# Wo's weight sums of two sets moved to other slots and all onto VectorE, one of them in a buffer of its own; low rank copies put in front of statistics at the end

## The chip, the cores and the metric

The kernel runs on one core of a Trainium2 chip. The metric is the device time of one execution in microseconds (us). An engine is called by its name in the profile: PE is TensorE, PEld its weight loads, DVE is VectorE, ACT is ScalarE, POOL is GpSimd, and SP is the engine that issues most DMAs.

## What is computed

One transformer layer with the norm after each part, in float32, on x of shape (2, 512, 512): grouped attention with 32 heads of 128 in 8 groups, then a linear layer with low rank experts.

```python
q = rope(x @ Wq + bq); k = rope(x @ Wk + bk); v = x @ Wv + bv
scores = where(causal, q @ k.T / sqrt(128), min)        # 4 heads share one k and v
x = layernorm(x + softmax(scores) @ v @ Wo + bo)
y = x @ W_base.T + b_base
z = einsum('bth,erh->bter', x, lora_A[active])          # 4 experts, rank 8
alpha = softmax(log(prior) + x @ router_W.T + router_b)[active]
x = layernorm(x + y + sum over experts of (z @ lora_B.T * 2) * alpha)
```

## The kernel before

**Units, parts and slots.** The attention is cut into 16 units, a unit being one group of four heads in one batch. A unit has four parts of 128 query rows. A part is worked in four steps of 32 rows by four heads, so one step is one score matmul of 128 rows against 32 to 512 keys. These 256 steps are the slots 0 to 255, and the width grows by 32 from slot to slot through the 16 slots of a unit (the last unit has its parts in another order). The order of every engine's instructions is written out by hand: `slot(T)` (from L960) issues what belongs to slot T, and at its end whatever `put(T, f)` (L868) has stored for that slot. Nothing reorders it later. Each engine runs its own queue in order, and waits at an instruction until what it needs is there.

In slot T, PE does a product of the projections of a later unit, a product of Wo for an earlier one, the score of step T (L552), and the weighing by v of a part some 12 slots back (L608). DVE does the masked maximum of step T-1 (L560), adds the Wo product that PE has just left in PSUM to x (L666, "x_sb<-wx" and "x_sb<-wy"), adds the q product (L480), and then the reciprocal, the 32x32 transposes (L583, L585) and a piece of the rotary embedding (L374, L377, L381). ACT does the exponential (L567) and the scaling (L575), and copies from PSUM. POOL does the last addition of the rotary embedding (L382) and sums of four matrix blocks (L427 to L430).

**Wo and its sums.** Products with Wo are done with seven block products in place of eight, the Strassen way. Besides the weights they need three sums of weight blocks and one block changed in place: `wo_sums(n, step)`, steps 0 to 3 (L627 to L634), each one instruction over 128x512 elements. Wo comes in sets of four heads, `load_wo(n)`, 1 MB, two buffers. There are ten sets. Sets 0 to 5 serve two units each; the sets 6 to 9 serve one unit each, and only 6 and 7 are multiplied this way (8 and 9 use plain matmuls, L680). The sums live in one buffer with the tag "wt". With `wo_from(u)` = 16u + 21, the first slot of unit u's Wo products, the four steps are put at offsets 0, 1, 1, 3 from there for the sets 0 to 5, all on DVE. For the sets 6 and 7 they are at offsets -1, 0, 0, 0, that is in slots 212 and 213, and 228 and 229, with steps 0 and 1 on DVE and steps 2 and 3 on POOL. The load of set 7 is issued at slot 214.

The two PSUM banks of the Wo products are "wx" and "wy". Each has one buffer, so PE can start the next product in a bank only after DVE has added the former one to x.

**The end.** From slot 237 the slots also hold the first half of the linear layer, for the token tiles of batch 0 (`f0[0]` to `f0[3]`). W_base is transposed on PE in four pieces through the one buffer of `ps_k`, each copied out by ACT (`transposed_base`, put at 241, 242, 245 and 246). After that come, for each tile: `base` (PE, L774), `logits` and `alphas` (a small softmax on DVE and ACT), `low_rank` (PE transposes 32 columns into the `ps_k` buffer, L810, and DVE copies them to zT, L811), `finish` (PE multiplies zT by the low rank factors, L815), `add` (DVE adds x, L821, and takes the statistics, L699 and L700), the square root on ACT (L707), the reciprocal on DVE (L710), and `store` (POOL applies the norm, L729, and SP issues the DMA). The tiles of batch 1 follow in straight code behind the slots: `fa` (two tiles), `fb` and `fc`. `fc` is worked in two halves of columns (`half`, L829), with statistics of each half (L839).

Of the kernel before, what the change touches and what calls it, by code (L numbers as in the profile page):

```python
# [9 lines left out]
F32 = mybir.dt.float32  # L10
# [5 lines left out]
P = 128  # L16
# [13 lines left out]
def postln_layer_kernel(  # L30
# [33 lines left out]
    nc = tc.nc  # L64
# [8 lines left out]
    EAR = EA * RK  # L73
# [14 lines left out]
    NSETS = len(sets)  # L88

    def unit(u):  # L90
        return units[u]

    def set_of(u):
        return u // B if u < MIXED else MIXED // B + u - MIXED

    def set_units(n):
        return [u for u in range(NU) if set_of(u) == n]
# [5 lines left out]
    wow = ctx.enter_context(tc.tile_pool(name="wow", bufs=2))  # L103
# [3 lines left out]
    ps_k = ctx.enter_context(tc.tile_pool(name="ps_k", bufs=1, space=bass.MemoryType.PSUM))  # L107
# [52 lines left out]
    def load_wo(n):  # L160
        wo_g = wow.tile([P, R, HID], F32, tag="wo_g", name=f"wo_{n}")
        nc.sync.dma_start(out=wo_g, in_=Wo[ts(sets[n], R * D), :].rearrange("(r p) n -> p r n", p=P))
        wos[n] = wo_g
# [113 lines left out]
    def transpose_token_tile(dst, src, pool, tag, copy):  # L277

        tp = pool.tile([P, KC, P], F32, tag=tag, name="tp")
        for c in range(KC):  # L280
            nc.tensor.transpose(tp[:, c, :], src[:, ts(c, P)], ident)  # L281
        copy(dst, tp)
# [127 lines left out]
    CH = KC // 2  # L410
# [192 lines left out]
    def weigh(p, j):  # L603
        u, i = parts[p]
        g, b = unit(u)
        if j == 0:
            psc[p] = ps_ctx.tile([P, R, P], F32, tag="ctx", name="pc")
        nc.tensor.matmul(  # L608
            psc[p], lhsT=v_sb[g // VG, b][:, j, ts(g % VG, D)], rhs=pT[p][:, :, ts(j, P)],
            start=(j == 0), stop=(j == i))  # L610
# [8 lines left out]
    NHALF = HID // 2  # L619
    wt = {}  # L620
# [3 lines left out]
    def wo_block(n, c_half, n_half):  # L624
        return wos[n][:, CH * c_half : CH * (c_half + 1), ts(n_half, NHALF)]

    def wo_sums(n, step, engine=nc.vector):  # L627

        if step == 0:
            wt[n] = wow.tile([P, 3, CH, NHALF], F32, tag="wt", name=f"wt_{n}", bufs=1)  # L630
        t1, t2, t4 = (wt[n][:, m] for m in range(3))
        b11, b12, b21, b22 = (wo_block(n, c_half, n_half) for c_half in range(2) for n_half in range(2))
        engine.tensor_tensor(
            *((t1, b12, b11), (t2, b22, t1), (b12, b22, b12), (t4, b21, t2))[step], ALU.subtract)  # L634

    def ctx_block(k, head, c_half):
# [38 lines left out]
    def wo_mm(p, r):  # L675

        u, i = parts[p]
        if r == 0:
            pwo[p] = ps_wo.tile([P, HID], F32, tag=("wx", "wy")[p % 2], name="po")
        nc.tensor.matmul(  # L680
            pwo[p], lhsT=ctxT[p][:, r, :], rhs=wos[set_of(u)][:, r, :], start=(r == 0), stop=(r == R - 1))

    def wo_out(p):
        u, i = parts[p]
        t = unit(u)[1] * TPB + i
        nc.vector.tensor_tensor(x_sb[:, t, :], pwo[p], x_sb[:, t, :], ALU.add)
# [52 lines left out]
    class Ffn:  # L739
# [29 lines left out]
        def base(self, c):  # L769
            if c == 0:  # L770
                self.new_banks()
            for n in range(2):
                w = OH + (ARH, WX_COLS - OH)[n]
                nc.tensor.matmul(  # L774
                    self.py[n][:, :w], lhsT=self.xT[:, c, :], rhs=wbT[:, c, n, :w], start=(c == 0), stop=(c == KC - 1),
                    skip_group_check=True)
# [28 lines left out]
                    ALU.mult,  # L805
                )

        def low_rank(self):
            tz = ps_k.tile([EAR, P], F32, tag="k", name="tz")
            nc.tensor.transpose(tz, self.zs.rearrange("p a r -> p (a r)"), ident)  # L810
            nc.vector.tensor_copy(self.zT[:EAR], tz)  # L811

# [4 lines left out]
                    skip_group_check=True)  # L817

        def add(self):
            for n in range(2):  # L820
                nc.vector.tensor_tensor(self.y[:, ts(n, OH)], self.py[n][:, :OH], self.x[:, ts(n, OH)], ALU.add)  # L821
            self.norm2.stats(self.i, self.y)

        def half(self, n, c):

# [42 lines left out]
    def put(slot, f):  # L868
        extra.setdefault(slot, []).append(f)
# [39 lines left out]
    late = {}  # L909
    PERIOD = VG * B * UNIT  # L910
    for p in range(1, G // VG):
        at = PERIOD * p
# [16 lines left out]
    def wo_from(u):  # L929
        return UNIT * u + LAG_WO  # L930

    for n in range(2, NSETS):
        put(wo_from(set_units(n - 2)[-1] + 1) + 1, lambda n=n: load_wo(n))
    for n in range(NSETS - 2):
        single = len(set_units(n)) == 1
        for k in range(4):
            put(wo_from(set_units(n)[0]) + ((-1, 0, 0, 0) if single else (0, 1, 1, 3))[k],
                lambda n=n, k=k, engine=nc.gpsimd if single and k > 1 else nc.vector: wo_sums(n, k, engine))


    weigh_at = {}
# [133 lines left out]
    T_PROJ = T_END - 19  # L1075
# [13 lines left out]
    QX, QY, SC, CTX = (ps_q, "qx"), (ps_q, "qy"), (ps_sc, "sc"), (ps_ctx, "ctx")  # L1089

    def tiles(ts_, banks, name):
        n = len(ts_)
        norms = Norm(ffn_pool, n, f"a{name}"), Norm(ffn_pool, n, f"f{name}")
        return [Ffn(t, bank, *norms, i) for i, (t, bank) in enumerate(zip(ts_, banks))]

    f0 = tiles(range(TPB), ((QX, QY), (QX, QY), (SC, SC), (QX, QY)), "0")
    fa = tiles([TPB + i for i in order[:2]], ((SC, SC), (WX, WY)), "1a")
# [5 lines left out]
    def transposed_base(c):  # L1103
        transpose_token_tile(wbT[:, :, c // 2, ts(c % 2, P)], wb_sb[:, c, :], ps_k, "k", nc.scalar.copy)

    for c in range(OC):
        put(T_PROJ + (0, 1, 4, 5)[c], lambda c=c: nc.sync.dma_start(out=wb_sb[:, c, :], in_=W_base[ts(c, P), :]))
        put(T_PROJ + (4, 5, 8, 9)[c], lambda c=c: transposed_base(c))
    put(A - 5, lambda: f0[0].norm1.newton(0, 2))
    for k, f in enumerate(f0):  # L1110
        put(A + (-7, -6, 0, 0)[k], f.stats)
# [2 lines left out]
        put(A + 1 + k // 2, f.centre)  # L1114
        put(A + 3 + k // 2, lambda f=f, k=k: f.transpose(*(QX, QY)[k % 2]))
    for f, at in zip(f0, (A + 5, A + 11, A + 13)):
        for c in range(KC):
            put(at + c // 2, lambda f=f, c=c: f.base(c))
        put(at + 2, lambda f=f: (f.logits(), f.alphas()))
        put(at + 3, f.low_rank)  # L1120
        put(at + 4, lambda f=f: (f.finish(), f.add()))
    put(E + 2, fa[0].stats)
    for T in range(T_PROJ, E + 7):
        slot(T)
# [10 lines left out]
    fa[0].norm1.root(0, 2)  # L1135
    for f in fa:
        f.centre()
    f0[0].norm2.root(0, 3)
    for f in f0[:3]:
        f.store()  # L1140
    for r in range(R):
        wo_mm(NP - 2, r)
    wo_out(NP - 2)
    base(fz)
    fb.stats()
    fb.norm1.root(0, 1)
    fb.centre()
    for j in range(2):
        weigh(NP - 1, j)
    context_out(NP - 1)  # L1150
# [25 lines left out]
    fa[1].logits()  # L1176
    fa[1].alphas()
    fa[0].finish()
    fa[0].add()
    fa[0].norm2.sqrt(0, 1)  # L1180
    for c in range(KC):
        fb.base(c)
        if c == 2:
            fa[1].low_rank()
    fc.low_rank()
    fa[0].norm2.invert(0, 1)
    fa[0].store()
    fb.logits()
# [4 lines left out]
    for c in range(KC):  # L1193
        fc.half(0, c)
    fc.half_end(0)
    fc.half_stats(0)
    fa[1].norm2.invert(1, 2)
    fa[1].store()
    fb.low_rank()
    for c in range(KC):  # L1200
        fc.half(1, c)
        if c == 1:
# [58 lines left out]
```

## Time and profile before

| | |
|---|---|
| median of three runs | 827.23 us (824.42, 827.23, 827.54) |
| profiled execution, its own time | 824.35 us |
| its span, first to last instruction | 822.4 us |
| busy: PE, PEld, DVE, ACT, POOL | 812.3, 598.2, 600.6, 379.3, 326.7 us |
| mean granted TensorE clock | 0.999 |
| DMA queue of SP | 114.98 MB, 48.5% of 16 engines' span |

A timeline row has the start, the duration (both in us), the engine, the line, the operation, the tile written and the tiles read, the shape, and how many instructions were merged. In brackets stands the idle time before it, if there was any, and what ended it. Ends of matmuls are modelled and overlap the start of the next one, so time that PE loses is best read from start to start: four matmuls over 256 columns take 0.86 us from their start to the start of the next group when nothing is waited for (the program issues two, the profile records four).

### The profile page before, as it was taken

The page shows a single profiled execution, that of the slowest core. Times are in us where ns is not written, and L with a number is a line of the kernel's source. Part 1 is how long each engine was busy: PE and PEld are TensorE (multiplying, and loading weights), DVE is VectorE, ACT ScalarE, POOL GpSimd, SP SyncE. Part 2 cuts the span into 40 slices and gives each one's busy share as a digit, 9 for nine tenths or more (in the row PEclk, how much of TensorE's full clock was granted, in tenths as well). Part 3 has the DMA queues.
Part 4 walks back from the last instruction along what each step waited for, and adds up shares of the span by engine and source line. Part 5 has one row for each costly group of instructions (what it writes and reads, how often), then busy time and mean ns, then how long its engine had stood idle before and what let it go on. Part 6 is the DMA issues. An engine that isn't in the chain of part 4 may idle for free.

```text
span 822.4 us, 11201 instructions
## 1 busy us (share of the span) xinstructions
PE 812.3 (99%) x3385; PEld 598.2 (73%) x3385; DVE 600.6 (73%) x1968; ACT 379.3 (46%) x1058; POOL 326.7 (40%) x381
## 2 busy tenths in 40 slices
PE   8999999999999999999999999999999999999997
PEld 5567777777777778777777878777877877556565
DVE  5368877677879876787868777787868779974455
ACT  1236453553545454444535454544545444563244
POOL 6464343512543445321443245353455535520033
PEclk9999999999999999999999999999999999999999
DMA  9015636445464637354454637365444626574211
GB/s 309 18 46 145 208 77 182 135 116 162 108 196 118 198 86 213 90 156 151 133 149 129 180 75 221 91 159 181 134 139 110 212 74 193 164 260 142 77 38 65
DMA packets 84414, 115.99 MB, mean 141 GB/s; under 512 B 6525, under 2 KB 64237, under 8 KB 82306
## 3 DMA queue, kind: packets, MB, share of 16 engines
q1 hardware_dynamic: 83682, 114.98, 48.5%
q8 instruction: 27, 0.44, 0.2%
q0 software_dynamic: 448, 0.14, 0.1%
q14 instruction: 33, 0.27, 0.1%
q10 hardware_dynamic: 224, 0.16, 0.1%
HBM read 71.21 MB, written 44.04 MB: 140 GB/s over the span
## 4 chain that ended last, share of the span: by engine, by line
PE 92%; DVE 5%; ACT 1%; POOL 1%; issue 1%; DMA 1%; SPq 0%; DVEq 0%; POOLq 0%
PE pc L608 16%; PE sc L552 14%; PE qx L440 11%; PE wx L440 11%; PE qy L440 9%; PE wy L440 8%; PE pp L361 5%; PE kx L440 4%; PE vx L518 4%; PE po L680 3%; PE py L774 3%; PE pv L344 3%; PE tp L281 1%; DMA x_sb<-_attn_hidden_states_dram 1%; DVE sc L560 1%
## 5 line engine op out<-in xcount | busy, mean ns | idle before, releaser
L567 ACT ACTIVATE p<-sc,nmax 128x288 f32<-128x288 f32 (+15 forms) x256 | 124.3, 486 | 205.4 <-DVE nmax L560 183.1
L560 DVE CUSTOM_DVE_ANT_0 sc<-sc,maskw 128x288 f32<-128x288 f32 (+15 forms) x256 | 114.3, 446 | 143.2 <-PE sc L552 141.6
L608 PE MATMUL pc<-pT,v 128*128 128x512 f32 x320 | 165.5, 599 | 0.0
L552 PE MATMUL sc<-kT,qT 128*128 128x160 f32 (+15 forms) x512 | 161.8, 398 | 0.2 <-ACT p L567 0.2
L382 POOL TENSOR_TENSOR qT<-q,t 128x512 f32<-128x512 f32 x56 | 77.0, 1375 | 176.0 <-DVE q L381 176.0
L575 ACT ACTIVATE p<-p,den 128x288 f32<-128x288 f32 (+15 forms) x256 | 133.2, 521 | 0.4 <-DVE den L571 0.3
L552 PEld LDWEIGHTS sc<-kT,qT 128*128 128x128 f32 x512 | 96.1, 190 | 23.1 <-issue 9.3
L615 ACT ACTIVATE ctxT<-pc,bqkT 128x512 f32<-128x512 f32 x64 | 44.0, 688 | 114.4 <-PE pc L608 114.4
L427 POOL TENSOR_TENSOR cs<-ctxT 128x256 f32<-128x256 f32 x28 | 22.4, 801 | 157.8 <-PE wy L440 93.7
L583 DVE STREAM_TRANSPOSE zt<-p 128x128 f32<-128x128 f32 (+2 forms) x192 | 81.6, 425 | 0.0
L608 PEld LDWEIGHTS pc<-pT,v 128*128 128x128 f32 x320 | 57.0, 190 | 19.1 <-issue 5.7
L440 PE MATMUL wx<-wo,ctxT 128*128 128x256 f32 x224 | 57.7, 380 | 0.7 <-DVE den L571 0.7
L440 PE MATMUL qx<-xs,wq 128*128 128x256 f32 x224 | 58.0, 381 | 0.0
L476 ACT COPY q<-qx 128x256 f32<-128x256 f32 x112 | 41.4, 369 | 35.8 <-PE qx L440 35.8
L440 PEld LDWEIGHTS qx<-xs,wq 128*128 128x128 f32 x224 | 41.4, 190 | 22.2 <-issue 18.4
L585 DVE STREAM_TRANSPOSE zt<-p 128x32 f32<-128x32 f32 (+3 forms) x256 | 57.5, 224 | 0.0
L567 ACT ACTIVATION_READ_ACCUMULATOR p<-sc,nmax 128x1 f32 x256 | 49.8, 195 | 0.0
L440 PEld LDWEIGHTS wx<-wo,ctxT 128*128 128x128 f32 x224 | 42.4, 190 | 8.7 <-issue 2.2
L374 DVE SCALAR_TENSOR_TENSOR t<-q,bqkT,rope_sb 64x512 f32<-64x512 f32 x56 | 46.3, 827 | 1.5
L666 DVE TENSOR_TENSOR x_sb<-wx,x_sb 128x256 f32<-128x256 f32 x112 | 47.0, 420 | 0.0
L377 DVE SCALAR_TENSOR_TENSOR t<-q,bqkT,rope_sb 64x512 f32<-64x512 f32 x56 | 42.5, 759 | 1.3
L571 DVE RECIPROCAL den<-den 128x1 f32<-128x1 f32 x256 | 39.3, 153 | 1.4 <-ACT p L567 1.2
(227 smaller groups left out, 1484.0 us busy)
## 6 DMA issues: line engine op xcount, KB each, us to landing
db<-zt SPq DMA_DIRECT2D x64, 256.0 KB, 4.2
pT<-db SPq DMA_DIRECT2D x16, 1024.0 KB, 4.8
db<-zt SPq DMA_DIRECT2D x64, 192.0 KB, 3.5
pT<-db SPq DMA_DIRECT2D x16, 768.0 KB, 4.5
wq<-in_L_attn_Wq_dram SPq DMA_DIRECT2D x20, 512.0 KB, 5.3
wo<-in_L_attn_Wo_dram SPq DMA_DIRECT2D x10, 1024.0 KB
db<-zt SPq DMA_DIRECT2D x64, 128.0 KB, 2.4
pT<-db SPq DMA_DIRECT2D x16, 512.0 KB, 4.1
```

Source lines behind the costliest of these rows:

```text
L374: nc.vector.scalar_tensor_tensor(t2[lo, :], q[hi, :], b_ap[hi, :], rope_sb[hi, 1, :], ALU.add, ALU.mult)
L382: nc.gpsimd.tensor_tensor(dst, t1[:, :].rearrange("p (n s) -> p n s", s=BLK), t2[:, :].rearrange("p (n s) -> p n s", s=BLK), ALU.add)
L440: nc.tensor.matmul(ps, lhsT=wt[:, c, :], rhs=xt[:, c, :], start=start and c == 0, stop=c == CH - 1, skip_group_check=True)
L552: nc.tensor.matmul(sc[s][:, :w], lhsT=qT[u][:, i * QB + n].rearrange("p r s -> p (r s)"), rhs=kT[u][:].rearrange("p n s -> p (n s)")[:, :w ...
L560: nc.vector.tensor_tensor_reduce(sc[s][:, :w], sc[s][:, :w], maskw[:, S - w :], -SCALE, -MASKED, ALU.add, ALU.min, nmax[s])
L567: nc.scalar.activation(ptile[s][:, :w], sc[s][:, :w], AF.Exp, bias=nmax[s], scale=-1.0, accum_out=rden[s])
L575: nc.scalar.activation(ptile[s][:, :w], ptile[s][:, :w], AF.Copy, scale=rden[s])
L583: nc.vector.transpose(z[:, :, last - i : last, n, :].rearrange("p q j s -> p j q s"), ptile[s][:, : i * P])
L585: nc.vector.transpose(z[:, : n + 1, last, n, :], ptile[s][:, i * P : w])
L608: nc.tensor.matmul(psc[p], lhsT=v_sb[g // VG, b][:, j, ts(g % VG, D)], rhs=pT[p][:, :, ts(j, P)], start=(j == 0), stop=(j == i))
L615: nc.scalar.activation(ctxT[p], psc[p], AF.Identity, bias=bqkT[:, col : col + 1])
L666: nc.vector.tensor_tensor(into, pw[k, bank], into, ALU.add)
```

## The change

The sums of the sets 6 and 7 are all done on DVE, like those of the others. Set 6 has its four steps 16, 15, 15 and 13 slots ahead of its products (slots 197, 198, 198 and 200), in a buffer of its own. Set 7 has them 11, 9, 6 and 5 slots ahead (slots 218, 220, 223 and 224), in the shared buffer "wt". Two of the four pieces of W_base are transposed one slot later. Of tile `f0[2]`, low rank comes a slot later, and its finish, sum and statistics come behind the slots, among the straight code. There, `f0`'s square root and stores move behind `fb.centre`. At the very end three copies of zT are moved in front of statistics on DVE, and `fc`'s small transpose uses the bank "ctx" in place of the `ps_k` buffer.

```diff
-    def wo_sums(n, step, engine=nc.vector):
+    def wo_sums(n, step):
         if step == 0:
-            wt[n] = wow.tile([P, 3, CH, NHALF], F32, tag="wt", name=f"wt_{n}", bufs=1)
+            shape = [P, 3, CH, NHALF]
+            if n == NSETS - 4:
+                wt[n] = late["pool"].tile(shape, F32, name="wt_late")
+            else:
+                wt[n] = wow.tile(shape, F32, tag="wt", name=f"wt_{n}", bufs=1)
...
-        engine.tensor_tensor(
+        nc.vector.tensor_tensor(
...
-        def low_rank(self):
-            tz = ps_k.tile([EAR, P], F32, tag="k", name="tz")
+        def low_rank(self, pool=ps_k, tag="k"):
+            tz = pool.tile([EAR, P], F32, tag=tag, name="tz")
...
         def add(self):
+            self.sum()
+            self.norm2.stats(self.i, self.y)
+
+        def sum(self):
             for n in range(2):
                 nc.vector.tensor_tensor(self.y[:, ts(n, OH)], self.py[n][:, :OH], self.x[:, ts(n, OH)], ALU.add)
-            self.norm2.stats(self.i, self.y)
...
     for n in range(NSETS - 2):
-        single = len(set_units(n)) == 1
+        at = {NSETS - 4: (-16, -15, -15, -13), NSETS - 3: (-11, -9, -6, -5)}.get(n, (0, 1, 1, 3))
         for k in range(4):
-            put(wo_from(set_units(n)[0]) + ((-1, 0, 0, 0) if single else (0, 1, 1, 3))[k],
-                lambda n=n, k=k, engine=nc.gpsimd if single and k > 1 else nc.vector: wo_sums(n, k, engine))
+            put(wo_from(set_units(n)[0]) + at[k], lambda n=n, k=k: wo_sums(n, k))
...
-        put(T_PROJ + (4, 5, 8, 9)[c], lambda c=c: transposed_base(c))
+        put(T_PROJ + (4, 6, 8, 10)[c], lambda c=c: transposed_base(c))
...
     for f, at in zip(f0, (A + 5, A + 11, A + 13)):
+        last = f is f0[2]
...
-        put(at + 3, f.low_rank)
-        put(at + 4, lambda f=f: (f.finish(), f.add()))
+        put(at + 3 + last, f.low_rank)
+        if not last:
+            put(at + 4, lambda f=f: (f.finish(), f.add()))
...
-    f0[0].norm2.root(0, 3)
-    for f in f0[:3]:
-        f.store()
     for r in range(R):
         wo_mm(NP - 2, r)
+    f0[2].finish()
     wo_out(NP - 2)
+    f0[2].sum()
     base(fz)
     fb.stats()
     fb.norm1.root(0, 1)
     fb.centre()
+    f0[2].norm2.stats(2, f0[2].y)
+    f0[0].norm2.root(0, 3)
+    for f in f0[:3]:
+        f.store()
...
     fa[0].finish()
-    fa[0].add()
-    fa[0].norm2.sqrt(0, 1)
+    fa[0].sum()
     for c in range(KC):
         fb.base(c)
         if c == 2:
             fa[1].low_rank()
-    fc.low_rank()
+    fa[0].norm2.stats(0, fa[0].y)
+    fa[0].norm2.sqrt(0, 1)
+    fc.low_rank(*CTX)
...
     fc.half_end(0)
-    fc.half_stats(0)
+    fb.low_rank()
     fa[1].norm2.invert(1, 2)
     fa[1].store()
-    fb.low_rank()
+    fc.half_stats(0)
```

## The prediction

> **What bounds the kernel now.** The page first: PE is busy 99% of the span at full clock, DVE 73%. The change removes no matmul, so it can only win time in which PE stands still. I looked for that in PE's timeline, from start to start. Between 560 and 680 us there is none to speak of. After 680 there is some, in four places. The largest is 697 to 701.
>
> ```profile
> PE 812.3 (99%) x3385; PEld 598.2 (73%) x3385; DVE 600.6 (73%) x1968; ACT 379.3 (46%) x1058; POOL 326.7 (40%) x381
> ```
>
> ```profile
> 697.25 0.59 PE L552 MATMUL sc<-kT,qT 128*128 128x256 f32 x2
> 697.93 1.13 PE L440 MATMUL wy<-wt,cs 128*128 128x256 f32 x4
> 698.90 0.65 PE L552 MATMUL sc<-kT,qT 128*128 128x288 f32 x2
> 699.39 1.02 PE L608 MATMUL pc<-pT,v 128*128 128x512 f32 x2
> 701.08 1.10 PE L440 MATMUL wx<-wo,ctxT 128*128 128x256 f32 x4 [0.67 <-DVE den L571]
> ```
>
> A score of width 256 needs 0.43 from start to start and took 0.68; wy needs 0.86 and took 0.97; pc needs 0.86 and took 1.69. Lost: 0.25 + 0.11 + 0.83 = 1.2 us. The DVE timeline of the same stretch says for whom PE waited:
>
> ```profile
> 690.04 1.22 DVE L633 TENSOR_TENSOR wt<-wo 128x512 f32<-128x512 f32 x1
> ...
> 692.72 1.16 DVE L377 SCALAR_TENSOR_TENSOR t<-kT,bqkT,rope_sb 64x512 f32<-64x512 f32 x1
> 693.90 1.65 DVE L633 TENSOR_TENSOR wt<-wo,wt 128x512 f32<-128x512 f32 x1
> ...
> 697.47 0.41 DVE L666 TENSOR_TENSOR x_sb<-wy,x_sb 128x256 f32<-128x256 f32 x1
> ...
> 698.52 1.61 DVE L374 SCALAR_TENSOR_TENSOR t<-q,bqkT,rope_sb 64x512 f32<-64x512 f32 x1
> ...
> 700.51 0.42 DVE L666 TENSOR_TENSOR x_sb<-wx,x_sb 128x256 f32<-128x256 f32 x1
> ```
>
> PE's wy (697.93) starts when DVE has emptied that bank (697.88), its wx (701.08) when DVE has emptied the other (700.93). DVE is late because it has had no pause since 688.67, with two sums of set 7 in the way, 1.22 and 1.65 us long. They take so long while POOL is busy: the shortest sum in the trace is 0.65.
>
> The third and fourth views are the timelines of PE and DVE at the end, for the small stalls there (below).
>
> **Set 7's sums (slots 218, 220, 223, 224).** Removed at 690 to 695 on DVE: 1.22 + 1.65 = 2.87 us, and POOL's two sums (1.72 each), beside which L374 took 1.61 against 0.75 elsewhere. DVE was 2.3 us behind PE's score at 700 (score ready 697.84, taken 700.16); 2.87 clears that, so the 1.2 us of PE go. What is late next? From 702 to 712 PE needs 10 us for slots 233 to 238 and DVE 9.2, so DVE keeps up. The later stall (0.30 at 714.7) stays: DVE's first statistics wait until 713.1 for a POOL addition that hangs on PE's own wy at 707.25, so it moves along with PE. Gain 1.20.
>
> Added: four sums on DVE earlier. Slots 218 and 220 end in pauses of 1.17 and 1.27 us with POOL idle or just starting, so 0.65 to 0.69 fits. At 223 and 224 the pauses are 0 and 0.16: two sums of 0.68 make DVE 1.16 us late at 681.2. Behind them are queued that slot's maximum, x_sb<-wy and the q sum (680.60, then 681.8). PE's next use of that q bank is at 683.59, 1.4 us after the sum would end; ACT's exponential is needed 3 us later. Pauses of 0.56 and 0.81 (682.9, 685.7) take the delay up again. POOL is idle from 674.9 to 682.5. Cost on PE 0. Without the pauses it would be 1.2. The first sum also waits for Wo's DMA, issued at 646.97: the DMA share falls from 1.01 to 0.05 at 655, five microseconds before the sum at 660.2. SP's queue is unchanged.
>
> **Set 6's sums (slots 197, 198, 198, 200).** Removed at 642 to 650: two DVE sums in slack and two POOL sums. PE lost nothing there, so gain 0. Its own buffer is needed since set 5's sums are still read; it adds no wait. Added: slot 198 takes two sums in a pause of 2.02 us, while POOL works from 598.8 to 606.5. The nearest row is set 5 in the same place of its cycle:
>
> ```profile
> 553.69 1.38 DVE L633 TENSOR_TENSOR wt<-wo,wt 128x512 f32<-128x512 f32 x1
> 555.00 1.21 DVE L633 TENSOR_TENSOR wo<-wo 128x512 f32<-128x512 f32 x1
> 556.13 0.39 DVE L560 CUSTOM_DVE_ANT_0 sc<-sc,maskw 128x224 f32<-128x224 f32 x1
> ```
>
> 2.59 us with POOL beside it: DVE takes the next score 0.55 late, and PE shows no gap from 546 to 562. This is where a rule speaks against the change. The Trainium skill (SBUF — State Buffer, "Who interferes with whom") says that a DVE instruction with two SBUF inputs and a GpSimd instruction that reads SBUF exclude each other, the later one blocked for the whole of the earlier; moving sums from POOL to DVE then buys no parallel work. By the rule I estimate each sum of slot 198 blocked by one POOL addition of 1.27: 0.65 + 0.68 + 2 x 1.27 = 3.9, DVE 1.9 late. By the row it is 2.6, DVE 0.6 late. PE's next wy is at 606.83 and DVE's add would end at 604.9 even by the rule. I take the row; the cost is 0 by both. By the same rule set 7 gains: its old sums met POOL's, its new ones mostly do not.
>
> **W_base one slot later.** Now PE waits 0.30 before the second transposition (720.98, for ACT's copy of the first) and 0.37 before the score at 722.69 (for ACT's exponential, itself behind that copy). With the transposition behind the score, the first stall goes, but the exponential comes no earlier: PE waits until 722.69 all the same, having less to do before. Then the transposition (0.43) comes on top, and the 0.18 lost at 725.0 for a transfer is filled. Sum +0.14. Bounds: -0.3 if ACT gives way, +0.43 if no gap is filled. The last piece moves where PE had no gap: 0.
>
> **f0[2].** Here PE waits for the small softmax:
>
> ```profile
> 776.55 1.02 PE L608 MATMUL pc<-pT,v 128*128 128x512 f32 x2
> 777.87 0.28 PE L810 MATMUL tz<-ident,zs 128*32 128x128 f32 x1 [0.30 <-DVE zs L801]
> ```
>
> pc should have handed over at 777.40, so 0.47 is lost. After the change po (1.72) comes first and zs is ready. Gain 0.47. The finish waits for zT at about 780.4, behind x_sb<-po on DVE; PE reaches it at 782.7. The moved statistics (0.69 + 0.18) and square root sit behind fb.centre: PE needs that tile's transpose at about 789, and DVE is some 2 us ahead. ACT's next exponential is at 793.07, behind copies. POOL's three applications (2.1 each) move from 785 to about 788, with three stores behind them that land 25 us before the end. Cost 0; if DVE were blocked by the last of them, a few tenths.
>
> **The last copies.** PE waits 0.26 before fc's tz (809.00, zT copied at 808.70 behind statistics) and 0.39 before fb's finish:
>
> ```profile
> 812.69 1.03 PE L829 MATMUL ph<-wbT,x1T 128*128 128x256 f32 x4
> 813.93 1.13 PE L815 MATMUL py<-bmT,zT 128*128 128x256 f32 x4 [0.21 <-DVE zT L811]
> ```
>
> The first goes. But the copy now in front must wait for PE's tz (807.73 + 0.31 = 808.04), so fa[0]'s statistics start at 808.24, not 807.87: 0.37 later. They carry the square root, ACT's table load (1.28) and fb's exponential (810.43 to 810.80), fb's zs, and fa[1]'s statistics. fb's copy then lands at 813.46 in place of 813.61. Gain 0.15; bounds -0.65 (both stalls) and +0.4 (the chain without the saving).
>
> **Sum.** -1.20 - 0.47 + 0.14 - 0.15 = -1.7 us. Against the profiled execution's 824.35 us (span 822.4 and 1.95 around it): 822.7. That execution lies at the low end of the runs; the same 1.7 off the median of 827.23 gives 825.5, which I predict.
>
> **Rivals.**
> 1. The relief is not passed on: at 697 to 701 DVE is still late for some other reason (L377 and L374 stay long because POOL's cs and kT additions remain), so only half of the 1.2 goes. For it: L377 at 692.72 took 1.16 without a sum on POOL. Against: even so DVE is 2.9 ahead. Sum -1.1, 826.1.
> 2. Slower, by the lock. The two sums in slots 223 and 224 have three pauses behind them, 0.16 + 0.56 + 0.81 = 1.53. If they cost more than this, DVE carries the delay into 688 to 701. At the longest durations of the trace, 1.65 + 1.75 = 3.4, it carries 1.9 of the 2.87 just freed, the 1.2 stays lost, and the q bank at 683.59 is freed some 0.6 late. Sum -0.47 + 0.14 - 0.15 + 0.7 = +0.2, 827.5. Against: POOL's idle 7.5 us there.
> 3. All bounds good: -1.2 - 0.47 - 0.3 - 0.65, and the rest of 712 to 726 eased by some tenths as DVE and ACT run ahead: -3, 824.2.
> 4. The change does less than it says: set 6's move and buffer are worth 0, since PE lost nothing there. This is in the forecast already.
>
> **How the numbers follow.** The forecast has 0.62, rival 1 0.15, rival 2 0.10, rival 3 0.13. All lie within 4 us of the start, and 0.5% (4.1 us) is about what a measurement of this kernel can tell from no change: the three runs spread over 3.1 us. So most of the chance is "same", 0.81. Faster needs 823.1: rival 3, or the forecast with its runs at the low end (824.42 - 1.7 = 822.7), 0.14. Slower needs 831.4, for which I have no mechanism: 0.05. The range takes the forecast from the lowest run, 822.2 with half a microsecond of the better bounds, to rival 2 with the same, 828.0.
>
> **What would show it.** In the profile after: no gap between pc and wx some 2 us after set 7's first products; DVE pausing for a score around 695; two sums in slot 198 near 2.6 us; two of 0.7 at about 677.4 and 680.5; PE waiting over 1 us before the 384 wide score at 721; no wait before f0[2]'s tz; fb's finish still waiting for zT. I am wrong if DVE is late at 681 by much over 1.2, or if PE's stall comes back behind the first statistics at 713.

## The result and the profile after

| | before | after |
|---|---|---|
| median, range | 824.51 us (823.83 to 827.54, 22 runs) | 823.12 us (822.45 to 826.92, 22 runs) |
| ratio of the times | | 0.9981, 95% interval 0.9973 to 0.9989 |
| profiled execution, its span | 824.35, 822.4 us | 822.99, 821.2 us |
| mean granted TensorE clock | 0.999 | 0.999 |

The change wins 0.19%, or 1.4 us; 1.7 was predicted. The interval leaves out 1, so the gain is clear of the noise, but it is small.

PE does the same matmuls and is busy for 1.7 us less, since their modelled ends hold some of the waits. DVE is busy for 3 us more, since it has taken the four sums over from POOL (page of after, part 1):

```profile
PE 810.6 (99%) x3385; PEld 598.5 (73%) x3385; DVE 603.7 (74%) x1972; ACT 379.2 (46%) x1058; POOL 320.9 (39%) x377
```

Busy time cannot say where the microseconds went, so I compare starts. The offset of a PE instruction is its start in a run less the start of the same instruction in before. If it falls between two instructions, PE has gained there. From 95 us to 692 the offset is constant to 0.01 in every run (+0.20 in after, from the start of the program): set 6's move gains and costs nothing. The rest, in us, with before's clock at the head:

| stretch | 692 to 702 | 702 to 716 | 716 to 726 | 751 to 789 | 789 to 803 | 803 to 816 |
|---|---|---|---|---|---|---|
| what lies in it | set 7's old sums | first wait at 714 | W_base | f0[2] | fz's softmax | last copies |
| predicted | -1.20 | 0 | +0.14 | -0.47 | 0 | -0.15 |
| after | -1.37 | -0.21 | +0.16 | -0.48 | **+0.39** | **+0.05** |

The sum is -1.46, with the 0.20 from the start -1.26, and the spans differ by 1.2. (Between 726 and 751 the offset changes by 0.01 at most in every run.)

**697 to 701.** PE's timeline of after, the rows that answer to the stalled ones of before:

```profile
697.34 0.59 PE L552 MATMUL sc<-kT,qT 128*128 128x256 f32 x2
697.77 1.03 PE L440 MATMUL wy<-wt,cs 128*128 128x256 f32 x4
698.64 0.65 PE L552 MATMUL sc<-kT,qT 128*128 128x288 f32 x2
699.12 1.02 PE L608 MATMUL pc<-pT,v 128*128 128x512 f32 x2
699.98 1.03 PE L440 MATMUL wx<-wo,ctxT 128*128 128x256 f32 x4
```

From start to start: 0.43, 0.87, 0.48, 0.86, each what it needs. The 0.67 in brackets at wx is gone. DVE, for which PE waited, in the same stretch of after:

```profile
693.95 1.48 DVE L381 SCALAR_TENSOR_TENSOR kT<-kT,bqkT,rope_sb 128x512 f32<-128x512 f32 x1
695.82 0.40 DVE L560 CUSTOM_DVE_ANT_0 sc<-sc,maskw 128x224 f32<-128x224 f32 x1 [0.39 <-PE sc L552]
...
698.33 0.42 DVE L670 TENSOR_TENSOR x_sb<-wx,x_sb 128x256 f32<-128x256 f32 x1
```

Now DVE waits for PE (0.39 at 695.82), as the prediction had it. It does so although L381 is still long beside POOL.

**The new places of the sums.** DVE in after, slots 223 and 224 (the first three rows), and slot 198:

```profile
677.63 0.69 DVE L637 TENSOR_TENSOR wo<-wo 128x512 f32<-128x512 f32 x1
680.70 0.69 DVE L637 TENSOR_TENSOR wt<-wo,wt 128x512 f32<-128x512 f32 x1
681.31 0.19 DVE L560 CUSTOM_DVE_ANT_0 sc<-sc,maskw 128x32 f32<-128x32 f32 x1
```

```profile
600.36 1.20 DVE L637 TENSOR_TENSOR wt_late<-wo,wt_late 128x512 f32<-128x512 f32 x1
601.49 1.21 DVE L637 TENSOR_TENSOR wo<-wo 128x512 f32<-128x512 f32 x1
602.62 0.39 DVE L560 CUSTOM_DVE_ANT_0 sc<-sc,maskw 128x224 f32<-128x224 f32 x1
```

Set 7's sums cost 0.69 each where POOL is idle; set 6's cost 2.4 for the two beside POOL. The row of set 5 had said 2.6, and the estimate by the rule of the exclusive lock 3.9. The estimate was too high, but the rule fits. POOL in the same stretch of after:

```profile
600.29 0.73 POOL L428 TENSOR_TENSOR cs<-cs,ctxT 128x256 f32<-128x256 f32 x1
601.10 1.05 POOL L429 TENSOR_TENSOR cs<-ctxT,cs 128x256 f32<-128x256 f32 x1
602.11 1.17 POOL L430 TENSOR_TENSOR ctxT<-ctxT,ctxT 128x256 f32<-128x256 f32 x1
```

The two engines take turns: they end at 601.02 (POOL), 601.56 (DVE), 602.15 (POOL), 602.70 (DVE) and 603.28 (POOL), each 0.54 to 0.59 after the other. So each waits for the whole of the earlier instruction. The estimate had put a POOL addition of 1.27 in front of each sum; those that stand there take 0.72 or 0.73 alone, as POOL's rows of before show at 600.44 and 601.12. PE shows no gap behind the sums of either set.

**719 to 724.** PE in after:

```profile
721.30 0.91 PE L552 MATMUL sc<-kT,qT 128*128 128x384 f32 x2 [0.97 <-ACT p L567]
722.05 0.60 PE L281 MATMUL tp<-ident,wb_sb 128*128 128x128 f32 x4
...
724.05 1.02 PE L608 MATMUL pc<-pT,v 128*128 128x512 f32 x2
```

The one long wait in front of the score is there (0.97 in brackets, 1.13 from start to start), the transposition behind it, and pc starts at once.

**fz's softmax, the part that was not predicted.** f0[2]'s tz starts at 777.90 with no wait. But 15 us later PE waits for another tz. All engines of after, 786 to 793:

```profile
786.39 6.21 POOL L733 TENSOR_SCALAR y<-y,mv_f,rstd_f 128x512 f32<-128x512 f32 x3 [54.63 <-DVE lg L791]
...
792.00 0.64 DVE L802 TENSOR_SCALAR al<-al,sm 128x4 f32<-128x4 f32 x1
...
792.98 0.28 PE L814 MATMUL tz<-ident,zs 128*32 128x128 f32 x1 [0.22 <-DVE zs L805]
```

The multiplication of four columns, "al", takes 0.64. It took 0.23 in before, where POOL's three applications had ended at 791.21, 2.5 us ahead of it. Now POOL ends at 792.60 and al ends at 792.64.

### The profile page after: what moved, and what is told of

Same layout as the page of the kernel before. It is cut to its first block, busy times and chain, and to the rows that moved or that the text cites. A ratio compares the mean times of both kernels' runs of the same rounds, so it can differ in the third digit from the quotient of the medians.

```text
span 821.2 us, 11196 instructions
## 1 busy us (share of the span) xinstructions
PE 810.6 (99%) x3385; PEld 598.5 (73%) x3385; DVE 603.7 (74%) x1972; ACT 379.2 (46%) x1058; POOL 320.9 (39%) x377
## 4 chain that ended last, share of the span: by engine, by line
PE 94%; DVE 3%; ACT 1%; DMA 1%; issue 0%; POOL 0%; SPq 0%; DVEq 0%; POOLq 0%
PE pc L608 16%; PE sc L552 14%; PE qx L440 12%; PE wx L440 11%; PE qy L440 9%; PE wy L440 9%; PE pp L361 5%; PE kx L440 4%; PE vx L518 4%; PE py L778 3%; PE po L684 3%; PE pv L344 3%; PE tp L281 1%; PE py L819 1%; DMA x_sb<-_attn_hidden_states_dram 1%; DVE st L703 0%
```

## The experiments

Each starts from after, unless said otherwise. The table gives its offsets by the same stretches (what PE lost or gained against before), and its time.

| | 692 to 702 | 702 to 716 | 716 to 726 | 751 to 789 | 789 to 803 | 803 to 816 | median us | ratio to before (95%) |
|---|---|---|---|---|---|---|---|---|
| after | -1.37 | -0.21 | +0.16 | -0.48 | +0.39 | +0.05 | 823.12 | 0.9981 (0.9973 to 0.9989) |
| e1 | 0 | 0 | +0.16 | -0.48 | +0.39 | +0.05 | 824.98 | 1.0006 (0.9997 to 1.0016) |
| e2 | -1.37 | -0.09 | +0.19 | -0.47 | +0.39 | +0.04 | 823.70 | 0.9996 (0.9987 to 1.0005) |
| e3 | -1.37 | -0.23 | +0.38 | 0 | -0.01 | 0 | 823.93 | 0.9997 (0.9988 to 1.0006) |
| e4 | -1.37 | -0.22 | +0.21 | -0.48 | 0 | +0.04 | 822.31 | 0.9972 (0.9962 to 0.9983) |
| e5 | -1.36 | -0.24 | +0.47 | -0.47 | +0.38 | +0.04 | 823.21 | 0.9983 (0.9974 to 0.9991) |
| e6 | 0 | -0.02 | +0.16 | -0.47 | +0.39 | +0.04 | 824.60 | 1.0001 (0.9989 to 1.0013) |
| e7 | -1.18 | -0.23 | +0.16 | -0.48 | +0.40 | +0.04 | 823.12 | 0.9985 (0.9977 to 0.9993) |
| e8 | -1.37 | -0.22 | +0.40 | -0.48 | 0 | -0.73 | 822.25 | 0.9971 (0.9959 to 0.9982) |
| e9 | -1.37 | -0.22 | +0.17 | -0.47 | -0.01 | -0.73 | 822.83 | 0.9980 (0.9968 to 0.9993) |
| e10 | -1.37 | -0.22 | +0.20 | -0.47 | -0.01 | -0.73 | 822.15 | 0.9974 (0.9965 to 0.9983) |

The intervals of the times are some 0.7 to 1 us to each side. What is smaller is read from the rows.

One loss is not in the table, since it lies behind PE's last product. In e1, e2 and e3 the span ends 6.7 to 6.9 us after the start of that product, in before, after and e4 to e7 6.0. In these three profiles a DMA packet of instructions (8 KB, 0.31 to 0.43 us) falls into the last store, the one that ACT issues, and the store's last packets end 2.2 to 2.4 us after the issue, against 1.6. I call this the late store. The times have it too: against the runs of before that were taken with them, they lie 0.4 to 0.8 us above the sums of their rows, where after and e4 to e7 lie between 0.3 below and 0.1 above. That the packet holds up the store is likely, but no run moves it away.

**e1: set 7's sums back.**

```diff
-NSETS - 3: (-11, -9, -6, -5)     # all on DVE
+NSETS - 3: (-1, 0, 0, 0)         # steps 2 and 3 on POOL
```

> The changed kernel with set 7's sums back in slots 228 and 229, steps 2 and 3 on POOL; set 6 and everything at the end stay changed. Theory (DVE, late by set 7's two sums, holds the banks that PE waits for): PE's stall at 697 to 701 comes back, 1.2 to 1.5 us over the changed kernel, so 824.4 to 824.6 on the scale of its median 823.12. Rival (set 6's move is the gain, or the end is): within 0.3 us of the changed kernel.

Measured: 824.98 us, above the 824.4 to 824.6 of the theory (the late store is in it), and the stalls at 697.08, 698.73 and 699.22 are back, with 0.68 for DVE in brackets at wx (700.91; 0.67 in before). All of -1.37 and of -0.21 goes with set 7's sums. What is left of the change is worth nothing or a loss: +0.16 + 0.39 + 0.05 - 0.48 = +0.12 by the rows (and 0.7 behind them).

**e2: half of set 7's sums back, those of POOL.**

```diff
-NSETS - 3: (-11, -9, -6, -5)     # all on DVE
+NSETS - 3: (-11, -9, 0, 0)       # steps 2 and 3 on POOL
```

> The changed kernel, but of set 7 only steps 0 and 1 are early on DVE (slots 218, 220); steps 2 and 3 are on POOL in slot 229 as before. DVE is relieved of 2.87 us, POOL of nothing. Theory (DVE's lateness alone): as the changed kernel within 0.3 us, no gap between pc and wx near 700. Rival (POOL's two sums, which hold DVE's rotary steps and delay POOL's own additions): 1.0 to 1.2 us over the changed kernel, the gap is back.

Measured: -1.37 in full, so what stopped PE was DVE being late by its own two sums. POOL's two cost 0.12 in the next stretch. The time, 823.70, is 0.6 over after's; the rows account for 0.15 of it, and the late store, 0.9 in its profile, more than covers the rest.

**e3: set 7's sums alone.** Before, with only set 7's sums in their new slots. Set 6's keep their slots and engines but have the buffer of their own, since set 7's first sum, at slot 218, would otherwise have to wait until PE has used set 6's.

```diff
...
+            if n == NSETS - 4:
+                wt[n] = late["pool"].tile(shape, F32, name="wt_late")
...
-        single = len(set_units(n)) == 1
+        at = {NSETS - 4: (-1, 0, 0, 0), NSETS - 3: (-11, -9, -6, -5)}.get(n, (0, 1, 1, 3))
+        on_pool = {(NSETS - 4, 2), (NSETS - 4, 3)}
...
```

> The kernel before with set 7's four sums moved as in the change; set 6's sums stay in their old slots and on their old engines and get the buffer of their own, without which set 7 could not start at 218; nothing at the end is changed. Theory: it has the whole of the 1.2 to 1.5 us, so 823.0 to 823.3 where before is 824.5, and the gap near 700 is gone. Rival (set 6's move shares the gain): half of it.

Measured: by the rows the theory. The -1.37 is whole, but +0.38 comes at W_base's old slots, so PE's last product comes 1.2 earlier (the start left out). By the time alone it would be the rival: 823.93 us where 823.0 to 823.3 was expected, and a span of 821.5, only 0.9 less than before. The late store takes 0.7 of what PE had won. Set 6's move itself is worth nothing; what set 7's early sums need is set 6's own buffer (by the order of the program: no run has set 7 early without it).

**e4: the stores of f0 split.** Two tiles' root and stores go back to the place that they had in before, and only f0[2]'s stays behind fb.centre.

```diff
-    f0[0].norm2.root(0, 3)          # behind fb.centre()
-    for f in f0[:3]:
-        f.store()
+    f0[2].norm2.root(2, 3)          # behind fb.centre()
+    f0[2].store()
...
+    f0[0].norm2.root(0, 2)          # in front of wo_mm(NP - 2, r)
+    for f in f0[:2]:
+        f.store()
```

> The changed kernel, with the square root, reciprocal and stores of f0[0] and f0[1] back where they were, in front of the last Wo products of part NP-2, and only f0[2]'s behind fb.centre. In the changed kernel PE waits 0.4 us for fz's tz near 793, for a 4 column DVE step that took 0.64 us while POOL applied the third norm. Theory (that DVE step is held up by POOL's norm): POOL is done by 789, the step takes 0.23, the wait goes, 0.3 to 0.4 us under the changed kernel. Rival (the wait hangs on ACT's copies and table load, which end with PE's transposes): the wait stays, same time within 0.1 us.

Measured: the +0.39 is gone, and nothing else has moved. All engines of e4, 786 to 793:

```profile
786.09 2.07 POOL L733 TENSOR_SCALAR y<-y,mv_f,rstd_f 128x512 f32<-128x512 f32 x1 [0.68 <-DVE lg L791]
...
791.71 0.23 DVE L802 TENSOR_SCALAR al<-al,sm 128x4 f32<-128x4 f32 x1
...
792.32 0.27 PE L814 MATMUL tz<-ident,zs 128*32 128x128 f32 x1
```

POOL has finished at 788.16, al takes 0.23, and tz does not wait. So PE's wait came from POOL's third application beside al and not from ACT's copies and table load, which have kept their places, and 822.31 us beats both kernels.

**e5: W_base back.**

```diff
-        put(T_PROJ + (4, 6, 8, 10)[c], lambda c=c: transposed_base(c))
+        put(T_PROJ + (4, 5, 8, 9)[c], lambda c=c: transposed_base(c))
```

> The changed kernel with the four pieces of W_base transposed in their old slots (241, 242, 245, 246). The prediction's account: the later slots cost PE 0.14, so this gains 0.1 to 0.2 us over the changed kernel. Rival, from the run with set 7 alone, where PE arrived early and then waited 0.56 for the transfer pT near 722 in place of 0.18: the later slots fill that wait with a transposition, and undoing them costs about 0.2.

Measured: +0.47 in place of +0.16. PE in e5:

```profile
722.71 0.86 PE L552 MATMUL sc<-kT,qT 128*128 128x416 f32 x2
724.05 1.12 PE L608 MATMUL pc<-pT,v 128*128 128x512 f32 x2 [0.47 <-DMA pT<-db]
```

This score needs 0.69 from start to start and takes 1.34: 0.65 lost to the transfer of pT, against 0.18 in before. SP's issue of that transfer has moved less than PE has: 1.15 earlier than in before (719.68 against 720.83), PE 1.59. In before, e3, e5 and e8, where PE waits for it, pc starts 4.34 to 4.38 after the issue. So a stall that set 7 removed comes back in part as a wait for a DMA, and a transposition in front of it fills that wait. With set 7's sums new, the old slots cost 0.38 (e3) and 0.47 (e5), the new ones 0.16 to 0.21 in six profiles and 0.40 in e8, where SP issued the transfer 0.3 later against PE than in e10, which has the same instructions there. With set 7's sums old, the new slots cost 0.16 (e1, e6). So they save some 0.2 in this company, with a scatter as large, and nothing that the times could show (823.21 against 823.12).

**e6: the end alone.** Both sets' sums are old, the end and W_base new.

```diff
-        at = {NSETS - 4: (-16, -15, -15, -13), NSETS - 3: (-11, -9, -6, -5)}.get(n, (0, 1, 1, 3))
+        at = {NSETS - 4: (-1, 0, 0, 0), NSETS - 3: (-1, 0, 0, 0)}.get(n, (0, 1, 1, 3))   # steps 2 and 3 on POOL
```

> The changed kernel with all of set 6's and set 7's sums, engines and buffer as before, so only the changes from slot 241 on remain. Theory: W_base +0.16, f0[2] -0.47, fz's tz +0.4 for POOL's moved stores, the end +0.05: 0.1 to 0.2 slower than before, 824.5 to 824.7. Rival (the prediction's sum of the same parts, -0.48): 824.0.

Measured: +0.10 by the rows, 824.60 us, ratio 1.0001. The prediction's -0.48 for these three edits together is refuted: f0[2]'s gain is spent 15 us later.

**e7: set 7's sums crowded.** Two in slot 223 and two in 224, to see from where rival 2 (slower, by crowding) would decide.

```diff
-NSETS - 3: (-11, -9, -6, -5)
+NSETS - 3: (-6, -6, -5, -5)
```

> The changed kernel with set 7's four sums in slots 223, 223, 224 and 224, so that 2.7 us of sums fall on DVE's three pauses of 1.53 us in all. By the prediction's second rival the remaining 1.2 us is carried into 688 to 701 and PE's stall comes back in part there, 0.3 to 0.8 us, and a bank of q or v near 683 to 686 is freed up to 0.6 late: 0.5 to 1.4 us over the changed kernel. The other view, that DVE has about 1.3 us of grace against PE's next use of each bank: only the q bank near 683.6 is late, by 0.2 to 0.4, and nothing at 697 to 701.

Measured: four sums of 0.69, 2.76 us where the three pauses hold 1.53. DVE takes the maximum of slot 224 at 682.18, 2.4 us later against PE than in before, and frees the q bank at 683.04, 0.3 ahead of PE's next use of it (683.32). PE loses only 0.19 between 692 and 702, and nothing at 683; neither forecast had this. The 0.19 is a wait for the transfer pT:

```profile
698.75 1.13 PE L608 MATMUL pc<-pT,v 128*128 128x512 f32 x2
```

SP issues that transfer at 693.92, 0.9 later against PE than in after, and it lands at 698.70. So rival 2's threshold of 1.53 is wrong as a price: what the pauses do not take up reaches PE through one transfer, as 0.19 of a microsecond, and no bank is late.

**e8: fb's copy in front of fa[1]'s statistics.** From e4, since in after PE still waits for zT. All engines of after, 808 to 813:

```profile
808.46 2.08 POOL L733 TENSOR_SCALAR y<-y,mv_f1a,rstd_f1a 128x512 f32<-128x512 f32 x1 [5.60 <-DVE lg L791]
...
810.10 0.46 DVE L802 TENSOR_SCALAR al<-al,sm 128x4 f32<-128x4 f32 x1
...
812.38 0.25 DVE L815 COPY zT<-tz 32x128 f32<-32x128 f32 x1
...
812.68 1.13 PE L819 MATMUL py<-bmT,zT 128*128 128x256 f32 x4 [0.51 <-DVE zT L815]
```

```diff
     fa[1].finish()
-    fa[1].add()
-    fa[1].norm2.sqrt(1, 2)
+    fa[1].sum()
...
     fb.low_rank()
+    fa[1].norm2.stats(1, fa[1].y)
+    fa[1].norm2.sqrt(1, 2)
```

> The kernel with the stores split, and at the very end fa[1]'s statistics also put behind fb's copy of zT. In the changed kernel PE waits 0.69 before fb's finish (812.68). Theory: the copy there is late because fa[1]'s statistics (0.69 and 0.18) stand in front of it, so it lands at 811.8 and PE waits 0.1 or so: 0.5 to 0.6 us under the kernel with the stores split. Rival: the copy is late because fb's small softmax hangs on ACT's table load, and the wait only shrinks by 0.1 to 0.2.

Measured: half of the theory. PE's wait is gone, and PE gains 0.73 in the last stretch, 0.77 more than in e4, but the time does not follow. Measured from 751 on, ACT's last application starts just 0.24 earlier than in e4 (816.36 against 816.71, of which 0.11 is a lower offset), and the time is the same, 822.25 against 822.31. On DVE, fb's sums start at 812.50, 1.28 after PE's start of that product, behind fa[1]'s reciprocal and fc's half statistics. The end hangs on DVE and ACT, not on PE.

**e9: fb's sums first.** From e8, with both of these behind fb's sums.

```diff
-    fa[1].norm2.invert(1, 2)
-    fa[1].store()
-    fc.half_stats(0)
     for c in range(KC):
         fc.half(1, c)
         if c == 1:
             fb.finish()
             fb.add()
+            fa[1].norm2.invert(1, 2)
+            fa[1].store()
+            fc.half_stats(0)
```

(f1[1], here and in e10, is fa[1].)

> As in e8, and besides f1[1]'s reciprocal and store and fc's half statistics are put behind fb's sums and statistics. Theory (the last part of the kernel is set by the chain on DVE and ACT from fb's sums to fc's last root, and not by PE): in e8 fb's sums start at 812.50, 0.4 us after PE has finished with the product at 812.08, since DVE has a reciprocal and a half statistic in front; they now start at about 812.1, the half statistic goes into the pause of 0.36 in which DVE waits for fb's root, and ACT's last application starts 0.35 earlier, at about 816.0 of the span with e8's start. Time about 821.9, which the times alone cannot tell from e8's 822.25; the rows can. Rival (another chain sets the end: the half statistic is needed in front of the last one, or POOL's application of f1[1], now at about 813.8 to 815.9, and its DMA end last): the last application starts where it did, or the last DMA does not end earlier; time 822.2 to 822.8.

Measured: the rival. This profile lost 3.6 us against e8's in its first 48 us (last section), so I count from PE's start of fb's low rank product (814.59; 811.22 in e8). fb's sums come at +0.63 (e8 +1.28), ACT's last application at +4.81 (e8 +5.14), 0.33 earlier as the theory said. But POOL's application of fa[1] now starts at 817.16, +2.57 (e8 +1.14). SP issues its store at 819.26, and fb's, ready since 818.79, behind it at 819.64; fc's last comes behind both (SP's queue in e9):

```profile
819.26 0.81 SPq L855 DMA_DIRECT2D out_dram<-y  x2
...
820.17 0.40 SPq L863 DMA_DIRECT2D out_dram<-y  x1
```

fc's half was ready at 819.82. Its issue is at +5.58, as in e8 (+5.59), so the 0.33 is lost in SP's queue. And with two stores just in front of it, it lands 2.57 us after its issue, against 1.73 in e8: the span ends at +9.43 (e8 +8.94).

**e10: the store kept early.** From e8, with only the half statistics moved.

```diff
     fa[1].norm2.invert(1, 2)
     fa[1].store()
-    fc.half_stats(0)
...
             fb.finish()
             fb.add()
+            fc.half_stats(0)
```

> As in e8, and besides only fc's half statistics are put behind fb's sums and statistics; f1[1]'s reciprocal and its store stay where e8 has them. Theory (e9 gained 0.33 on the chain of DVE and ACT to the last application, measured from PE's finish of fb, and gave it back because POOL's application of f1[1] started 2.57 us after PE's finish of fb rather than 1.14 and SP's queue put its two DMA issues in front of fc's): with that store kept early, fb's sums start about 0.7 to 0.9 after PE's finish of fb rather than 1.28, the last application some 0.3 earlier than in e8, SP's last issue too, and the span ends 0.3 earlier against the same start: about 821.9. Rival (the end hangs on something else, such as the two last transfers sharing the DMA engines, or ACT's root for f1[1] holds DVE as long as the half statistic did): the last application or the landing is not earlier, 822.2 to 822.5.

Measured: the theory. PE's offsets from 751 to the end are those of e8 within 0.04. The rows of e10, all engines, at the end:

```profile
812.14 0.73 DVE L829 TENSOR_TENSOR y<-py,x_sb 128x256 f32<-128x256 f32 x2
...
815.99 0.56 ACT L741 ACTIVATE y<-ph,shift,rstd_f1c 128x256 f32<-128x256 f32 x1 [0.42 <-DVE shift L740]
816.44 0.33 SPq L863 DMA_DIRECT2D out_dram<-y  x1
```

The sums, the last application and SP's last issue are 0.36 or 0.37 earlier than in e8, and the span is 819.8 in place of 820.2. The median is 822.15 us. The times do not tell e4, e8 and e10 apart (ratios 0.9972, 0.9971, 0.9974); all three beat both kernels.

## Why the prediction held, point by point

**Set 7's old sums, -1.20: right, -1.37.** Cause and place are shown by e1 (undone) and e3 (alone); e2 shows that DVE's own two sums did it. The term was 0.17 low: it was summed from three gaps, and 0.11 more goes at wx in front of them (696.3 to 696.6 in before), by the offsets.

**"The later stall (0.30 at 714.7) stays": wrong, small.** It shrank by 0.2. By e2, 0.12 of this comes from taking the two sums off POOL; through which row the rest comes was not settled.

**Set 7's new places at 0: right, with a larger margin than was argued.** e7 puts twice as many sums into the slots 223 and 224 for 0.19.

**Set 6 at 0: right; the estimate by the rule was mis-sized.** 2.4 us for two sums, no PE gap. The prediction set the row against the rule, but they do not differ. The Trainium skill (SBUF — State Buffer, "Who interferes with whom") calls the ports that DVE and POOL share an exclusive lock, and these sums did wait for whole additions of POOL: 1.20 where they take 0.69 alone. The 3.9 came from additions of 1.27 where additions of 0.73 stand, and from adding whole durations where the later instruction ends 0.55 after the earlier.

**W_base, +0.14: the number right (+0.16), the comparison wrong.** The terms that the prediction names give 0.43 - 0.18 = +0.25; to come to +0.14 the wait for pT must count as nearly 0.3, and the offsets of after do show 0.28 filled there (0.17 in front of pc, 0.11 within it). And it was worked out on before's timeline, and so on before's waits. In the timeline that set 7's move leaves, the old slots cost 0.38 to 0.47 (e3, e5): in this company the new slots save some 0.2. A wait for a DMA had grown behind the stall that was removed.

**f0[2], -0.47: right; "POOL's three applications ... Cost 0": the step that failed.** It cost 0.39. I had checked what hangs on the stores, which land far from the end, and not which DVE instructions lie beside POOL in the new place. "If DVE were blocked by the last of them, a few tenths" was named and then put at 0. e4 takes the three applications apart and the 0.39 is gone.

**The last copies, -0.15: +0.05, by the same cause, as the rows have it.** The delay of the chain by 0.37 came as predicted: DVE's wait for fb's exponential went from 0.92 to 1.29. But al took 0.46 and not 0.23, beside POOL's application of fa[0]. -0.15 + 0.23 = +0.08. No run takes this overlap away by itself. (Two copies of zT stand in front of statistics now, not three: fa[1]'s and fb's. fc's is still behind those of fa[0].)

**The sum and its base.** With the two terms at al, -1.7 would have been -1.7 + 0.39 + 0.23 = -1.1; the larger gains at 692 to 716 (-0.38) bring it back to -1.46. So the total is nearer than its terms by luck: the errors cancel. The point of 825.5 was 2.4 too high because 1.7 was taken off the median of three runs, 827.23; 22 runs put it at 824.51, and the profiled execution's 824.35 would have led to 822.7.

**Rivals.** The first (half passed on) and the second (slower by crowding) did not come; e7 shows that the second's threshold was far too low. The third (all bounds good) is not reached by this change, but e10, at -2.3 us, comes near it. The fourth is right for set 6, except that its buffer is what lets set 7 move.

## What to carry to other kernels

Work that is moved is priced by what runs beside it in its new place: look up which instructions of the other engine (DVE and POOL held each other up here) fall into that window, even those of 0.2 us, if the bottleneck waits behind them. When an early stall goes, work out the later edits on the timeline that remains, since waits for transfers grow where the bottleneck arrives earlier than their data. At the very end of a kernel follow the last output back through each queue it passes, SP's among them: PE ending 0.7 earlier brought 0.24, and a store moved behind it took away 0.33 won elsewhere.

## What the runs showed of the hardware

**A sum on DVE and an addition on POOL exclude each other.** In all twelve profiles, a weight sum on DVE (128x512, 0.68 to 0.69 us with POOL idle) that starts while POOL is in an addition ends 0.54 to 0.55 us after that addition (9 to 15 cases in each profile). An addition of POOL that starts during such a sum ends 0.58 to 0.59 us after it at 128x256 (0.72 to 0.73 alone) and 1.12 to 1.14 at 128x512 (1.26 to 1.27 alone). So the later one does nearly its whole work behind the earlier. In the one pair of each profile that starts within 0.02 us, DVE goes first.

**A small DVE instruction held until POOL is done.** The 128x4 multiplication al lasts 0.23 us alone. In the ten profiles with after's order of the last copies (after and all experiments but e3) fb's al falls beside fa[0]'s application on POOL, and each time takes 0.46 and ends 0.02 us after POOL. Beside the third application of f0, in the six profiles without e4's split, fz's al takes 0.64 and ends 0.02 to 0.03 after POOL. The rule of the Trainium skill (SBUF — State Buffer, "Who interferes with whom"), that a tensor_scalar on DVE can take both port pairs and that then, of it and an instruction of POOL, the later one waits for all of the earlier, fits these. It does not fit before, where fb's al began 1.28 us into POOL's 2.08 and took 0.23 (in e3 it was the same, 1.27 and 0.23):

```profile
809.77 2.08 POOL L729 TENSOR_SCALAR y<-y,mv_f1a,rstd_f1a 128x512 f32<-128x512 f32 x1 [5.62 <-DVE lg L787]
...
811.05 0.23 DVE L798 TENSOR_SCALAR al<-al,sm 128x4 f32<-128x4 f32 x1
```

In after the held ones began 1.46 and 1.64 us into POOL's. Whether POOL holds the ports only in its last part, or its recorded times are off (they are rough), no run here settles.

**PE's first matmuls, slow in one execution.** e9's profiled execution took 825.78 us where its median is 822.83. Against before it is 3.18 us late at 48 us, and still 3.18 late at 692; from there on its offsets follow e10's within 0.04. The eight matmuls of the first k projection, before and e9 (lowest, median and highest duration in ns, first and last start):

```profile
L361 PE MATMUL pp<-xT,wk x8: 592/592/697, 8.2 to 11.3; 128*128 128x512 f32 x8
```

```profile
L361 PE MATMUL pp<-xT,wk x8: 592/1057/1219, 9.1 to 14.5; 128*128 128x512 f32 x8
```

In e9 most of them ran at about half the speed, and so did their weight loads (median 332 ns against 190), until 13.7 us. The clock row of the profile shows 1.00 there, but only because it counts time without a clock record as full: the trace's first clock record, of full clock, starts at 5.1 us in before and at 13.7 in e9. PE's 128-column transposes say the same: in before they start 0.21 us apart up to 4.97 and 0.11 from 5.17 on, in e9 0.21 apart up to 8.0. The Trainium skill (TensorE: Matmul & The Clock Gate, Part 1) has PE start at half its clock for a time that varies from run to run, and these records agree with that. The time is longer than the some 3.4 us of sustained work that the page names: full clock came in e9 12.5 us after PE's first matmul (1.19), with pauses of PE between. Whether the high runs of the other kernels have this cause is not known, as only one profile of such a run exists.
